# A two-layer convolution kernel on Trainium2: reordering the passage from the last attention region to the last convolution stage

## The chip, the cores and the metric

The kernel runs on one core of one Trainium2 chip. Its metric is the device time of a whole execution, in microseconds; lower is better. The core has TensorE (PE) for matrix products, VectorE (DVE), ScalarE (ACT) and GpSimd (POOL) for the rest, SyncE (SP) that mostly issues transfers, and 16 DMA engines that move data between HBM and the on-chip memory.

## The reference, cut to what matters

The input x is (4, 128, 128, 128): four images, 128 channels, 128 x 128 pixels, float32. Layer 0 is region attention followed by a convolutional MLP:

```python
reg = x[:, :, ih, iw]                       # 9 x 9 overlapping regions of 16 x 16 pixels, step 14
y = _ln(tok, ln1_g, ln1_b); qkv = y @ w_qkv # per region
attn = softmax(q @ k^T * hd ** -0.5)        # 4 heads of 32
tok = attn @ v @ w_out + b_out + tok
merged = out / cnt                          # regions added back, seams divided by their count
xf = merged                                 # (b, h*w, c)
y = _ln(xf, ln2_g, ln2_b) @ w_p0 + b_p0     # 128 -> 256 channels
ym = depthwise 5x5 convolution of y
ym = batchnorm(ym)                          # statistics over all images and pixels
y = gelu(gelu(ym)) @ w_p2 + b_p2 + xf
```

Layer 1 is two 3x3 convolutions of quantised activations and weights, each with a batch norm, and a residual. It is not touched by the change.

## The kernel before, in words

**Tiling.** Each image is nine bands of sixteen rows (two of them shared with the next band), so there are T = 36 bands over four images. One pass of the loop over t works on one band of nine regions: slot j = 0 to 8 runs the scores, exponentials and values of region j, and lists beside them pieces of other work. These are the first norm and projections of a later band (`ln1_chunks`, called a1 and a2), the tail of the band before (`post_chunks`, b1 and b2: output projection `wo`, residual, second norm, the projection `wp0` called p0 in lines L511 and L640, and the stores of its result y), and steps of an earlier image's 5x5 depthwise convolution. `beside(t)` returns the plan: which of these pieces stand in which slot. PE, ACT, DVE and SP run their instructions exactly in the order in which the program lists them; only POOL's order is left to a scheduler.

**A tail.** `post_begin` (L592, L593, L595) adds and halves the seams of the band's attention output `ob`. `project` multiplies by `wo` (L511) and adds the residual into `xf` (L622). The norm squares on ACT (L444), sums over channels on PE (L450), forms the variance (ACT L456, DVE L457, and L460, which clips it at zero), takes Ln and Exp on ACT (L464, L465), spreads the result over all channels and multiplies on DVE into `xn` (L494). In most tails the spreading goes through a DMA; in the last one it is four products with a selector matrix on PE (L477), which `selector` (L429) copies from the identity. Four p0 pieces for each block, one for each half of the channels (h) and of the rows (hh), multiply by `wp0`. ACT evicts each into a y tile with even and odd columns taken apart (L640), of which there are two for each h, used in turn, and SP stores it to `y_d` in HBM (L504). A y tile is free again when its store has landed.

**The last attention band** (t = T-1 = 35). After its nine slots the loop lists the last region's values (L952, L960 on PE, reciprocal L972 and products L974, L976 on DVE, the seam's addition L979 on POOL), then `post_begin` on DVE, then the p0 pieces left over from the previous band's second block, and then the tail of the last band by `beside(T)`.

**The late stage** (`conv_rest`, L773). The rest of the last image's depthwise convolution is 24 tiles. A tile takes input rows u from `y_d` in up to eight row groups: one main transfer on SP and two halo transfers on POOL (`fill`, L692), and its band matrices w by POOL (L667). Input tiles are three from the attention stage (`ut_`), three new ones (`ur`) and one of the `ob` tiles, so seven tiles are loaded ahead. What doesn't depend on the last tail is loaded before `beside(T)`, the remaining row groups after it. Each tile's products (L678) go to two score banks in PSUM, used in turn; ACT copies each half to a `cr` tile (L821), DVE takes its batch-norm statistics from `cr` (L827), and SP and ACT store one half each to `cv_d` (L830). After the fourth tile from the end SP issues `first_loads`: for the first two units of the gelu stage, 1 MB of `cv` (L199) and 0.5 MB of `xfl` (L206) each. When the last tile is copied, DVE aggregates the statistics (L184) and forms the batch norm's scale and shift (L1114 to L1120), and ACT begins with gelu (L1304).

Of the kernel before, what the change touches and what calls it, by code (L numbers as in the profile page):

```python
# [48 lines left out]
def layers(  # L49
# [56 lines left out]
    vectors, used = const.tile([P, 25], F32, name="vectors"), [0]  # L106
# [16 lines left out]
    eps_t, mhalf, qb, quad = vectors[:, 17:18], vectors[:, 18:20], vectors[:, 20:21], vectors[:, 21:25]  # L123
    nc.vector.memset(eps_t, LN_EPS)
# [70 lines left out]
    def load(n):  # L195
        b, k = pixel_units[n]
        cv = ld[0].tile([P, 2, U], F32, name="cv")
        src, px = (cv_d[b][k // 2], pixels(k % 2)) if b < B - 1 else (cv_d[b], pixels(k))
        nc.sync.dma_start(out=cv, in_=src.rearrange("(h p) n -> p h n", p=P)[:, :, px])  # L199
        loaded[n] = [cv]  # L200

    def load_xf(n):
        b, k = pixel_units[n]
        xf = ld[0].tile([P, U], F32, name="xfl")
        if b < B - 1:
            nc.sync.dma_start(out=xf, in_=xf_d[b][:, pixels(k)])  # L206
        else:
            nc.sync.dma_start(
# [5 lines left out]
    def first_loads():  # L214
        for n in range(2):
            load(n)
            load_xf(n)

    with ExitStack() as actx:
# [205 lines left out]
        def selector(room):  # L425
# [3 lines left out]
            nc.vector.tensor_copy(  # L429
# [4 lines left out]
        def normalise(src, n, sel=None):  # L434
# [11 lines left out]
            def variance():  # L446
# [9 lines left out]
                nc.scalar.activation(rstd, ps[:, 0, :w], AF.Square, scale=1.0 / P)  # L456
                nc.vector.scalar_tensor_tensor(  # L457
# [41 lines left out]
        def store(out, in_):  # L499
            stores.append((out, in_))  # L500

        def flush(n, engine=nc.sync):
            for out, in_ in stores[:n]:
                engine.dma_start(out=out, in_=in_)  # L504
# [81 lines left out]
        def post_begin(t, engine=nc.gpsimd):  # L586
            b, i = bands[t]
            rows = RS if i == NR - 1 else STEP

            o = ob[t]  # L590
            if i:
                engine.tensor_tensor(o[:, 0:2, :], o[:, 0:2, :], ob[t - 1][:, RS - 2 :, :], ALU.add)  # L592
                engine.tensor_scalar(o[:, 0:2, :], o[:, 0:2, :], 0.5, 1.0, ALU.mult, ALU.mult)  # L593
            seam = o[:, :rows, STEP : STEP * NR].rearrange("p r (j c) -> p r j c", c=STEP)[:, :, :, 0:2]
            engine.tensor_scalar(seam, seam, 0.5, 1.0, ALU.mult, ALU.mult)  # L595
# [8 lines left out]
        def post_chunks(t, sel=None):  # L604
# [4 lines left out]
            for at, (r, n) in enumerate(finished(t)):  # L609
# [24 lines left out]
                def p0(h, hh, r=r, n=n // 2, held=held):  # L634
# [3 lines left out]
                    y = y2t[h].pop(0)  # L638
                    y2t[h].append(y)
                    nc.scalar.activation(  # L640
                        y[:, :n],
                        pm[:, : n * P].rearrange("p (r c e) -> p r e c", r=n, e=2),
                        AF.Identity, bias=bp0[:, h : h + 1],
                    )
                    cut = min(n, GR - (row + 2) % GR)
                    for a, z in ((0, cut), (cut, n)):
                        if z > a:
# [3 lines left out]
                                y[:, a:z].rearrange("p r e x -> p (r e) x"),  # L651
                            )
# [120 lines left out]
        def conv_rest(n, pool, next_loads):  # L773
# [11 lines left out]
            U, W = {}, {}  # L785
# [13 lines left out]
            us += [pool.tile([P, 32 * CW], F32, name=f"ur{n_}") for n_ in range(3)]  # L799
            us.append(op.tile([P, RS, P], F32, name="ob").rearrange("p r c -> p (r c)"))  # L800
            ws += [pool.tile([P, 3, 8, 32], F32, name=f"wr{n_}") for n_ in range(3)]

            for at in range(ahead):
                if at >= len(ut_):
                    nc.gpsimd.memset(us[0], 0.0)
                if tiles[at][2] == 0 and len(W) >= len(wt_):
                    nc.gpsimd.memset(ws[0], 0.0)
                begin(at)
                load(at, 0, tiles[at][3] - 1, halo=False)
                load(at, 0, tiles[at][3] - 2, main=False)  # L810
            for t in ws[: len(ws) - len(W)]:
                nc.gpsimd.memset(t, 0.0)

            def step(at):
# [3 lines left out]
                depthwise(pc, W[k, jj][:, :, c:], U[at], 4 * nj)  # L818
                for half in range(2):
                    cv = pool.tile([P, nj * ng, CW], F32, name="cr", bufs=7)  # L820
                    nc.scalar.copy(  # L821
                        cv.rearrange("p n x -> p (n x)"), pc[half].rearrange("p j g x -> p (j g x)")
                    )
# [675 lines left out]
```

## Time and profile before

| | us |
|---|---|
| median of 3 runs | 3064.66 (3064.0 to 3068.08) |
| profiled execution | 3063.26 |
| its span, first to last instruction | 3061.5 |
| PE busy | 2951.9 (96%) |
| DVE busy | 2023.4 (66%) |
| ACT busy | 1986.0 (65%) |
| POOL busy | 1025.5 (33%) |

The mean clock granted to PE is 0.988 of full speed. Times inside the kernel are counted from the start of the span. The page cuts the span into 40 slices of 76.5 us and gives a digit for each engine and slice, the busy share in tenths; the passage of which this document speaks lies from about 1984 to 2125 us, most of it in the slices that begin at 1990 and 2066 us. A timeline line gives start and duration of a group of instructions, engine, line of the kernel, operation, tiles, and in brackets how long the engine was idle before it and what ended the wait. A window line gives busy time and instruction count of PE, weight loads, DVE, ACT and POOL, the PE clock, the mean busy share of the DMA engines and GB/s.

### The profile page before, as it was taken

How to read it: one execution, taken by the hardware profiler on the slowest of the kernel's cores; microseconds unless marked ns; L12 is line 12 of the kernel's file. 1: busy time of each engine (PE TensorE's matmuls, PEld its weight loads, DVE VectorE, ACT ScalarE, POOL GpSimd, SP SyncE). 2: the span in 40 equal slices, each digit the busy share in tenths (PEclk: the TensorE clock that was granted, in tenths of full speed). 3: DMA queues.
4: the chain of work that ended last, by engine and by line, in shares of the span. 5: the costliest groups of instructions: out<-in, count | busy, mean ns of one | idle time of the engine just before them, and what ended most of it. 6: DMA issues, size and time to landing. Idle time of an engine off the chain costs nothing.

```text
span 3061.5 us, 87377 instructions
## 1 busy us (share of the span) xinstructions
PE 2951.9 (96%) x36860; PEld 1406.8 (46%) x36860; DVE 2023.4 (66%) x3184; ACT 1986.0 (65%) x2643; POOL 1025.5 (33%) x1370
## 2 busy tenths in 40 slices
PE   7999999999999999999999999977999999999998
PEld 4545554444444444444444444533444444444443
DVE  4877898777777777776676667735555555666543
ACT  5778787777777777777766677634677666333343
POOL 5444445444444444444344444452111111000000
PEclk9999999999999999999999999989999999999999
DMA  7455776777776677777688787789999997551498
GB/s 164 130 154 171 187 186 176 204 220 221 210 215 188 181 213 213 214 220 203 175 237 237 207 229 207 224 269 314 359 359 358 356 340 234 165 158 43 163 360 302
DMA packets 720636, 686.14 MB, mean 224 GB/s; under 512 B 512065, under 2 KB 599434, under 8 KB 712554
## 3 DMA queue, kind: packets, MB, share of 16 engines
q1 hardware_dynamic: 701802, 644.90, 69.8%
q0 software_dynamic: 12832, 28.74, 3.3%
q10 hardware_dynamic: 5600, 6.80, 0.6%
q8 instruction: 293, 4.80, 0.6%
q14 instruction: 109, 0.89, 0.1%
HBM read 408.72 MB, written 275.51 MB: 223 GB/s over the span
## 4 chain that ended last, share of the span: by engine, by line
PE 82%; DMA 5%; DVE 4%; ACT 4%; issue 3%; POOL 1%; SPq 1%; ACTq 0%; DVEq 0%; POOLq 0%
PE pc L1267 22%; PE pm L511 18%; PE sc L889 9%; PE po L952 9%; PE pm L678 9%; PE pb L1316 7%; PE po L960 4%; PE pm L450 3%; DMA y_d<-y 2%; DVE rd L972 2%; ACT pt L897 1%; ACT v L880 1%; DVE xn L494 1%; DVE xf L622 0%; DMA u<-in_L_conv_w_dram 0%
## 5 line engine op out<-in xcount | busy, mean ns | idle before, releaser
L972 DVE RECIPROCAL rd<-po 128x256 f32<-128x256 f32 x324 | 568.8, 1755 | 386.1 <-PE po L960 382.5
L897 ACT ACTIVATE pt<-sc 128x1024 f32<-128x1024 f32 x648 | 628.4, 1025 | 119.1 <-PE sc L889 63.0
L1267 PE MATMUL pc<-q,wq 128*128 128x512 fp8e4 x3168 | 699.2, 380 | 5.1 <-DVE q L1279 5.1
L907 POOL TENSOR_TENSOR sm<-pt 128x512 f32<-128x512 f32 x324 | 414.7, 1280 | 673.4 <-ACT pt L897 451.4
L1267 PEld LDWEIGHTS <-wq 128*128 128x128 fp8e4 x3168 | 309.1, 98 | 405.6 <-issue 42.4
L889 PE MATMUL sc<-q,kr 32*128 32x256 f32 x5184 | 389.6, 402 | 17.7 <-ACT pt L897 17.2
L889 PEld LDWEIGHTS sc<-q,kr 32*128 32x128 f32 x5184 | 241.1, 183 | 271.9 <-issue 181.7
L952 PE MATMUL po<-pt,v 128*32 128x256 f32 x5184 | 350.3, 388 | 9.8 <-DVE part L976 9.0
L678 PE MATMUL pm<-u,w 64*32 64x504 f32 (+3 forms) x5376 | 290.2, 558 | 0.0
L907 DVE TENSOR_TENSOR sm<-pt 128x512 f32<-128x512 f32 x324 | 249.0, 768 | 22.3 <-ACT pt L897 22.3
L511 PE MATMUL pm<-xn,wqkv 128*32 128x512 f32 (+1 forms) x2304 | 247.1, 551 | 1.8
L511 PE MATMUL pm<-xn,wp 128*32 128x512 f32 (+1 forms) x2304 | 241.5, 548 | 7.1 <-ACT y L640 4.4
L640 ACT ACTIVATE y<-pm,vectors 128x512 f32<-128x512 f32 (+1 forms) x288 | 182.8, 641 | 93.9 <-PE pm L511 54.8
L1316 PE MATMUL pb<-cv,wp 128*128 128x512 f32 x512 | 233.6, 599 | 8.4 <-ACT cv L1307 8.4
L1275 DVE BATCH_NORM_STATS2 st<-pc 128x6 f32<-128x512 f32 x256 | 165.8, 690 | 84.2 <-PE pc L1267 84.2
L742 ACT COPY c<-pm 128x512 f32<-128x512 f32 x208 | 111.9, 590 | 164.7 <-PE pm L678 164.5
L952 PEld LDWEIGHTS po<-pt,v 128*32 128x32 f32 x5184 | 138.2, 109 | 174.7 <-issue 81.0
L979 POOL TENSOR_TENSOR ob<-ob,part 128x32 f32<-128x32 f32 x288 | 128.7, 447 | 229.7 <-DVE part L976 216.7
L960 PE MATMUL po<-sm,ones 128*32 128x256 f32 x2592 | 203.6, 382 | 1.9 <-POOL sm L907 1.9
L1329 POOL TENSOR_SCALAR a<-y 128x1024 f32<-128x1024 f32 x64 | 66.5, 1039 | 394.3 <-DVE y L1324 394.3
L1324 DVE SCALAR_TENSOR_TENSOR y<-pb,vectors,xfl 128x512 f32<-128x512 f32 x128 | 90.3, 747 | 140.9 <-PE pb L1316 136.1
L511 PE MATMUL pm<-wqkv,yr 128*32 128x128 f32 x5184 | 176.7, 274 | 0.0
(186 smaller groups left out, 3730.6 us busy)
## 6 DMA issues: line engine op xcount, KB each, us to landing
cv<-cv_d SPq DMA_DIRECT2D x64, 1024.0 KB
u<-y_d SPq DMA_DIRECT2D x96, 560.0 KB
cv_d<-c SPq DMA_DIRECT2D x208, 256.0 KB
xn<-row SPq DMA_DIRECT2D x76, 512.0 KB
y_d<-y SPq DMA_DIRECT2D x136, 256.0 KB
xfl<-xf_d SPq DMA_DIRECT2D x64, 512.0 KB
id_d<-y SPq DMA_DIRECT2D x64, 512.0 KB
idt<-id_d SPq DMA_DIRECT2D x64, 512.0 KB
```

Of the source, the lines that this page charges most:

```text
L511: nc.tensor.matmul(out[m], w[:, m], v, start=True, stop=True)
L640: nc.scalar.activation(y[:, :n], pm[:, : n * P].rearrange("p (r c e) -> p r e c", r=n, e=2), AF.Identity, bias=bp0[:, h : h + 1],)
L678: nc.tensor.matmul(outs[half][32 * q : 32 * q + 32, j, :, a:z], wt[hs, s, c, :], ut[hs, :, c, a + s - 1 : z + s - 1], start=(s == 1), stop ...
L889: nc.tensor.matmul(sc[h // 2][:, h % 2, kc, :].rearrange("p (r c) -> p r c", c=RS), region(kr, j)[hs, kc * P : (kc + 1) * P], queries(j, h ...
L897: nc.scalar.activation(pt, sc[p], AF.Exp)
L907: add(sm, pt[:, :, 0, :], pt[:, :, 1, :], ALU.add)
L952: nc.tensor.matmul(po[hs, 0, :], v[:, kc, hs], pt[h // 2][:, h % 2, kc, :], start=(kc == 0), stop=(kc == 1),)
L960: nc.tensor.matmul(po[hs, 1, :], ones, sm[h // 2][:, h % 2, :], start=True, stop=True)
L972: nc.vector.reciprocal(rd, po[:, 1, :])
L1267: nc.tensor.matmul(pc[:, h], w[:, t, :], q1[b][:, rows, dx : dx + P], start=(t == 0), stop=(t == 8),)
L1275: nc.vector.bn_stats(st[:, 2 * n + h, :], pc[:, h])
L1316: nc.tensor.matmul(pb[:, m], wp2[:, h, :], cv[:, h, px], start=(h == 0), stop=(h == 1))
```

## The change

It has seven parts.

1. In the last region (t = 35, j = 8), the first two p0 pieces of the first block stand ahead of `values(8)`, and `post_begin` follows on DVE; then come the scaling of the second block's xn, the other two p0 pieces, and the second block's. The seam's addition of this region is done by DVE. In this band the convolution step of slot 8 stands in slot 4.
2. `post_begin` on DVE halves by a tensor_tensor with a vector of 0.5. Where the selector is used, variance and square of the mean are put into a maximum in PSUM, and then subtracted, in place of a subtraction and a maximum with zero; the selector is copied by ACT.
3. In the last tail, the p0 pieces with hh = 1 have y tiles of their own (pool `rp`, name `xr`). Those with h = 1 are evicted by DVE and stored through ACT's queue, those with h = 0 as before.
4. The loads of the first three late tiles that don't depend on the last tail are issued in slot 8 (`first`), those of tiles 3 to 6 before the last tail (`more`). Of the first three, two of the row groups remain for afterwards, of the others one.
5. The statistics of the late stage are taken from the score bank in PSUM.
6. The last three late tiles are copied into input tiles that are spent.
7. `first_loads` is issued through ACT's queue ahead of the late stage's products.

```diff
             o = ob[t]
             if i:
...
-                engine.tensor_scalar(o[:, 0:2, :], o[:, 0:2, :], 0.5, 1.0, ALU.mult, ALU.mult)
+                halved(o[:, 0:2, :])
...
+                if sel is not None:
+                    nc.vector.scalar_tensor_tensor(
+                        ps[:, 1, :w], ps[:, 1, :w], 1.0 / P, rstd, ALU.mult, ALU.max
+                    )
+                    nc.vector.tensor_tensor(rstd, ps[:, 1, :w], rstd, ALU.subtract)
+                    return
...
+            def halved(part):
+                if engine is nc.gpsimd:
+                    engine.tensor_scalar(part, part, 0.5, 1.0, ALU.mult, ALU.mult)
+                else:
+                    spread_ = [[0, n] for n in part.shape[1:]]
+                    half = bass.AP(phalf.tensor, phalf.offset, [phalf.ap[0], *spread_])
+                    engine.tensor_tensor(part, part, half, ALU.mult)
...
+                    if t == T - 1 and hh:
+                        if h == 0:
+                            held["y"] = rp.tile([P, LB * P], F32, name="xr")
+                        y = held["y"][:, h * LB * P // 2 : (h + 1) * LB * P // 2].rearrange(
+                            "p (r e x) -> p r e x", r=RB, e=2
+                        )
+                    else:
+                        y = y2t[h].pop(0)
+                        y2t[h].append(y)
...
+                    bias, engine = bp0[:, h : h + 1], nc.sync
+                    if t == T - 1 and h:
+                        engine = nc.scalar
+                        nc.vector.tensor_scalar(y[:, :n], by_column, bias, None, ALU.add)
+                    else:
+                        nc.scalar.activation(y[:, :n], by_column, AF.Identity, bias=bias)
...
+            open_ = lambda at: 2 if at < len(ut_) else 1
+
+            def first(at):
+                begin(at)
+                ng = tiles[at][3] - open_(at)
+                load(at, 0, ng, halo=False)
+                load(at, 0, ng - 1, main=False)
...
+                    if at < len(tiles) - 3:
+                        cv = late["pool"].tile([P, 8 * CW], F32, name="cr", bufs=7)
+                    else:
+                        spent = done[at - 3].rearrange("p g c x -> p (g c x)")
+                        cv = spent[:, half * 8 * CW : (half + 1) * 8 * CW]
+                    pc_ = pc[half].rearrange("p j g x -> p (j g x)")
+                    nc.scalar.copy(cv, pc_)
...
-                            st0[:, k, half, at_, unit, :], cv[:, 4 * j : 4 * j + 4].rearrange("p n x -> p (n x)")
+                            st0[:, k, half, at_, unit, :], pc_[:, 4 * CW * j : 4 * CW * (j + 1)]
...
-                    if at == len(tiles) - 4:
-                        next_loads()
...
             if t == T:
                 return [
                     *b1[:2], *b2[:2], b1[2], b1[3], b2[2], b2[3], b1[4], b2[4],
-                    b1[5], b2[5], b1[6], *b1[7:], b2[6], *b2[7:],
+                    b1[5], b1[6], b2[5], b2[6], *b1[7:], *b2[7:],
                 ]
...
+            if t == T - 1:
+                order = (1, 5, 3, 7, 4, 6, 2, 0)
...
+                    if t == T - 1 and j == NR - 1:
+                        first, more, rest = conv_rest(len(units) - 1)
+                        for at in range(len(ut_)):
+                            first(at)
+                        halves(j)
+                        values_in(j)
+                        run([*side[2][:2], side[1][1]])
+                        values(j)
+                        post_begin(t, nc.vector)
+                        run([side[1][0], *side[2][2:]])
+                        break
...
-            last()
             flush(len(stores))
-            post_begin(T - 1, nc.vector)
...
-            rest = conv_rest(len(units) - 1, late, first_loads)
-            run(beside(T, selector(late.tile([P, 4 * P], F32, name="sel"))))
+            more(late)
+            run(beside(T, selector(late.tile([P, 4 * P], F32, name="sel"), nc.scalar.copy)))
             flush(len(stores))
+            first_loads()
             rest()
```

## The prediction

> **What bounds the kernel now.** I read the page's engine table and slices first, then the chain that ended last around the place of the change, then engine timelines, the table of waits and the windows there. The page says that the span is TensorE's (PE), except near 2000-2030 us:
>
> ```profile
> PE 2951.9 (96%) x36860; PEld 1406.8 (46%) x36860; DVE 2023.4 (66%) x3184; ACT 1986.0 (65%) x2643; POOL 1025.5 (33%) x1370
> PE   7999999999999999999999999977999999999998
> PE 82%; DMA 5%; DVE 4%; ACT 4%; issue 3%; POOL 1%; SPq 1%; ACTq 0%; DVEq 0%; POOLq 0%
> ```
>
> Each slice is 76.5 us; the two 7s (1990-2143 us) are the passage from the last attention region through the last tail to the late stage's convolution. All that the change moves lies there, so I work on that stretch alone. The timelines of DVE, then ACT, then PE (start, duration, idle before and its releaser) show three stalls:
>
> ```profile
> 1995.61 0.30 DVE L595 TENSOR_SCALAR ob<-ob 128x256 f32<-128x256 f32 x1
> 2001.51 3.26 DVE L460 TENSOR_SCALAR rstd<-rstd 128x256 f32<-128x256 f32 x1
> 2005.13 0.50 DVE L460 TENSOR_SCALAR rstd<-rstd 128x256 f32<-128x256 f32 x1
> ...
> 2004.81 0.51 ACT L464 ACTIVATE rstd<-rstd,vectors 128x256 f32<-128x256 f32 x1 [1.70 <-DVE rstd L460]
> 2020.33 0.69 ACT L640 ACTIVATE y<-pm,vectors 128x512 f32<-128x512 f32 x1 [4.05 <-DMA y_d<-y]
> 2115.83 1.07 ACT L821 COPY cr<-sc 128x512 f32<-128x512 f32 x2 [5.62 <-DMA xfl<-xf_d]
> ...
> 1996.05 3.64 PE L511 MATMUL pm<-ob,wo 128*32 128x512 f32 x32 [1.83 <-DVE ob L595]
> 2005.82 6.13 PE L477 MATMUL pm<-rstd,sel 128*128 128x256 f32 x16 [3.16 <-ACT rstd L465]
> 2011.88 6.22 PE L511 MATMUL pm<-xn,wp 128*32 128x512 f32 x56
> 2029.45 10.79 PE L678 MATMUL sc<-u,w 64*32 64x512 f32 x138 [6.45 <-DMA u<-y_d]
> ```
>
> One L460 takes 3.26 us where its twin takes 0.50. A y eviction waits 4.05 us for a store to free its tile. The last two copies of the convolution wait 5.62 us behind the first loads of the gelu stage. The convolution starts at 2029.45, when the last y store has landed (2026.97 on the chain) and a halo load, 2.0-2.1 us to landing, has followed it. Then the windows, whose last columns are clock, DMA share and GB/s:
>
> ```profile
> 2016.00:2020.00 4.00, 2.10 (x20) 0.39 (x12) 0.00 (x0) 0.28 (x1) 0.00 (x0) 1.00 1.05 318
> 2020.00:2024.00 4.00, 1.94 (x8) 0.20 (x8) 0.00 (x0) 2.75 (x4) 0.00 (x0) 0.62 0.93 226
> 2024.00:2028.00 4.00, 0.00 (x0) 0.00 (x0) 0.00 (x0) 0.00 (x0) 0.73 (x2) 0.50 0.66 166
> 2028.00:2032.00 4.00, 2.55 (x21) 0.58 (x29) 0.00 (x0) 0.00 (x0) 4.00 (x8) 0.50 0.50 141
> 2032.00:2036.00 4.00, 4.00 (x64) 1.40 (x56) 0.00 (x0) 0.36 (x1) 3.51 (x8) 0.67 0.22 60
> 2036.00:2040.00 4.00, 4.00 (x85) 1.50 (x72) 2.61 (x8) 1.78 (x4) 1.57 (x3) 1.00 0.73 228
> 2044.00:2048.00 4.00, 4.00 (x112) 2.12 (x103) 3.87 (x16) 1.43 (x3) 2.09 (x5) 1.00 1.05 360
> ```
>
> The DMA engines are full up to 2024, have a hole of about 7.6 us (4 x (0.34 + 0.50 + 0.78 + 0.27)) from 2024 to 2040, and are full again up to 2104, where tiles come every 3.6 us against 2.55-2.8 us of PE work. So the stage is bound by transfers on both sides of the hole.
>
> **What the Trainium skill says.** "SBUF — State Buffer", Who interferes with whom: a tensor_scalar on DVE can take a port pair that it shares with GpSimd, and whoever comes second waits for the other's whole instruction; an operation with at most one SBUF input outside these modes doesn't. The trace agrees: POOL (GpSimd) is busy 4.00 of 4.00 us in 2000-2004, with memsets and descriptors, and L460 takes 3.26. "DMA: Bandwidth & Descriptors", Issuing engines are not separate DMA queues: SP and ACT feed the same 16 engines; and Queues, rings and completion order there: each engine goes round-robin between its queues by packets. No stretch of this trace shows two large queues side by side. Its Specifications put line rate at 512 bytes or more: the y stores, rows of 256 bytes, run at 226 GB/s with DMA 0.93 busy, the convolution's loads at 360. "TensorE: Matmul & The Clock Gate", What's actually happening: after some idle windows the clock halves; here it is 0.50 in 2024-2032.
>
> **The change part by part**, against the profiled execution (3063.26 us, 3061.5 of span and 1.76 around it; the runs have a median of 3064.66, 1.4 above it).
>
> *Listing of the last region.* values(8) goes ahead of two of b1's p0 (16 matmuls at 6.22/56 = 0.111 us, 1.8), so it ends near 1989.7 instead of 1991.46, where the other block's p0 begin. DVE follows with rows of before: reciprocal 1.74, products 0.39 and 0.18, seam 0.3 (now DVE), post_begin 0.43 + 0.29 + 0.30, then xn 0.69: 4.3 us, and 0.4 of handovers, to 1994.4. PE has the two p0 until 1991.5, waits 2.9, then does the other block's four p0 (2.7, as at 1991.46-1994.2 before) and comes to wo at 1997.1 instead of 1996.05: **+1.1**, bounds -1.8 (the wait for L595 gone, nothing in its place) and +2. The convolution step that moves from slot 8 to 4 is 2.7-2.8 us of PE in a stretch where PE has no idle, here as there: 0, bounds -1 and +1.
>
> *rstd.* Max and subtract now read PSUM, so one SBUF input each; 0.42 as L457. ACT, in order, has its second L456 until 2003.10, so L464 starts there instead of 2004.81: **-1.7**. If the shorter idle keeps the clock from falling at 2003.9, L477 (6.13 us at half speed) takes about 3: bound -4.7. The selector's copy on ACT (0.42 on DVE) falls in ACT's idle of 3.49 us before L444: 0; without that cover, 0.4.
>
> *y in own tiles, two engines, two queues.* Removes the 4.05 us. p0 starts at 2011.88 + 1.1 - 1.7 = 2011.3; 64 matmuls at 0.111 are 7.1 us, the last eviction (0.69) ends near 2019.2 instead of 2023.81: -4.6. What is late next is the store's landing. The stores are 2 MB, at 226 GB/s 9.2 us of full DMA; from the first issue (2013.7) with some 2 us to land that is 2025 at the earliest, while prefetches still share the engines. So at most 2 of the 4.6 us arrive.
>
> *First loads.* cv and xfl for two units (3 MB) are issued by ACT right behind its y stores, and the built program puts the third unit's cv (1 MB) on SP ahead of the remaining main rows of the first convolution tiles, its xfl behind them: 4.5 MB in all, at 360 GB/s 12.5 us of DMA. Before they ran at 2105-2124, beside the convolution's end. The hole holds 7.6 us. ACT's loads take packets from the last y stores: landing moves from a possible 2025 to 2025-2030, I take 2027.5, which is +0.5 on 2026.97. Then tile 0's remaining rows queue on SP behind 1 MB that shares with ACT: 5.5 us at half of 360 GB/s, of which 2-3 are over before the y landing. The first convolution matmul comes near 2031.8: **+2.3** on 2029.45 (this holds the three parts above). Behind it on SP: the third xfl waits for ACT's second, and the first result's store and tile 7's load come after it. The load of 4.5 MB is through by about 2038, so the full DMA period starts later by these 2.3 us and isn't longer. Bounds: 2025 for the stores with the loads covered, -4.6; uncovered, 12.5 - 7.6 + 2.3 = +7.
>
> *The in-chain issue* of the first three tiles' loads: before they were issued at 1989-2005, and DMA was 0.88-1.04 busy there apart from 2000-2004 (0.53). 0; bounds -1.9 (that gap filled) and +0.5.
>
> *Statistics from PSUM.* Copy and bn_stats now read one bank and alternate by program order: 0.58 + 0.75 + 0.58 + 0.75 and handovers, about 2.9 us from a tile's last matmul until its bank is free, where the copies alone took 1.07. Under tiles 3.6 us apart that is hidden; the last four at 2.55-2.6 lose 0.3 each: **+1.2**, bounds 0 and 24 x 0.35 = 8.4 if no tile were bound by DMA.
>
> *End of the convolution.* The last tiles go to spent buffers and no load stands before their stores. Before: last matmul 2111.64, last bn_aggr 2119.1, 7.5 us. After: 2.9 + 1.32 (L184) = 4.2: **-3.3**, bounds -4.5 and -2. The chain from there to gelu (BN affine, 5.5 us from L184 to L1304) is unchanged, and its ACT table load (1.28) lies beside DVE's work.
>
> Sum: 2.3 + 1.2 - 3.3 = **+0.2**, 3063.5 on the profile; on the median of the runs about 3064.9; I say 3065.
>
> **The rivals.** *Loads hidden, landing early:* the hole takes all, the stores land at 2025 and the SP load is over by then, first matmul 2027 (-2.4), or 2025 with the clock kept (-4.6); with -3.3 and no loss in the banks, -5.7 to -7.9: about 3058. For it: 7.6 us of hole, 18 us between 2020 and 2038. Against: stores at 226 GB/s. *Slower:* the 4 MB ahead on two queues starve the 256-byte stores and the first tiles' rows, which PE waits for; at 1 packet of 4 KB to one of 256 bytes the stores land only when ACT's loads (8.3 us) are through, 2030-2032, and the SP load follows: first matmul 2036-2039, +7 to +10, sum +5 to +8, 3070-3073. It decides from a first matmul later than 2037.7, where the sum passes +6.1. For it: each of the stores' packets is small, and several SP issues also wait for ACT's transfers. Against: half of the stores are issued before the loads. *Moved wait only:* the rows of the stall vanish and the store wait reappears before the convolution, its start within 1 us of before; then -2 from the last copies, 3062.7. This counts as no change.
>
> **How the numbers follow.** The measurement can tell about 0.2% (6.1 us). My forecast has 0.42 and the moved wait 0.13. Loads hidden has 0.22, of which 0.16 passes -6.1. Starved stores have 0.23, of which 0.22 passes +6.1 (the bound of the banks, 8.4, counted there). What doesn't pass joins the middle: 0.16 / 0.62 / 0.22. The range leaves out about 0.1 at either end: 3057.5, nearly the hidden case, to 3074, starved stores and banks together.
>
> **What would show it.** L460 gone and the new pair at 0.3-0.6 us; no y eviction waiting on a store; wo's wait at 2.5-3 us behind xn; first convolution matmul near 2031.8 waiting for a load behind cv; DMA share 0.9 and more over 2024-2036; ACT copies alternating with bn_stats; the last bn_aggr about 4.2 us after the last matmul. The forecast is wrong if the first matmul stands before 2027 or after 2037, or if the convolution's tiles are further apart than 3.6 us.

## The result and the profile after

The changed kernel takes 3079.97 us (median of 6 runs, 3074.51 to 3081.03) against 3066.04 us for the kernel before, measured beside it (6 runs, 3062.22 to 3068.4): a ratio of 1.0044, 95% interval 1.0031 to 1.0057. It is about 14 us slower. Its profiled execution took 3080.01 us with a span of 3078.1.

The page of the changed kernel, the lines that answer to those shown of before (busy time and share of each engine; PE's busy tenths in 40 slices; shares of the chain that ended last):

```profile
PE 2954.3 (96%) x36860; PEld 1408.6 (46%) x36860; DVE 2025.9 (66%) x3189; ACT 1984.9 (64%) x2640; POOL 1025.1 (33%) x1369
PE   7999999999999999999999999967999999999998
PE 82%; DVE 5%; DMA 5%; ACT 4%; issue 3%; SPq 0%; POOL 0%; ACTq 0%; DVEq 0%; POOLq 0%
```

PE has the same work; a 7 became a 6. The timeline of PE in the changed kernel (start, duration, in brackets the idle time before and its releaser; L519 was L511, L485 was L477, L704 was L678):

```profile
1997.98 4.48 PE L519 MATMUL pm<-xn,wp 128*32 128x384 f32 x32 [2.87 <-issue]
2003.74 2.78 PE L519 MATMUL pm<-ob,wo 128*32 128x512 f32 x24 [0.42 <-ACT y L669]
2010.84 3.72 PE L485 MATMUL pm<-rstd,sel 128*128 128x256 f32 x16 [1.35 <-ACT rstd L473]
2014.49 7.07 PE L519 MATMUL pm<-xn,wp 128*32 128x512 f32 x64
2045.49 4.93 PE L704 MATMUL sc<-u,w 64*32 64x512 f32 x48 [23.93 <-DMA u<-y_d]
```

The last p0 ran without a stop (7.07 us for 64 matmuls), and ended at 2021.57 against 2023.00 before. Then PE stood still for 23.93 us: the late convolution began at 2045.49, not 2029.45. To compare executions without what differs earlier (2.5 us here), I count from the first exponential of the last band (1939.06 us before, 1941.57 after):

| us from the first exponential of the last band | before | after | difference |
|---|---|---|---|
| last wo begins | 57.00 | 60.68 | +3.7 |
| last p0 ends | 83.95 | 80.00 | -4.0 |
| first late convolution matmul | 90.39 | 103.92 | +13.5 |
| last late convolution matmul | 172.58 | 187.26 | +14.7 |
| last bn_aggr ends | 180.03 | 191.42 | +11.4 |
| first gelu | 185.56 | 197.19 | +11.6 |
| end of the span | 1122.40 | 1136.55 | +14.2 |

So the loss lies between the last p0 and the first late matmul: 6.45 us before, 23.93 after. The end of the convolution gave 3.3 us back. The 2.5 us between gelu and the end are not in all executions of kernels with the same gelu stage (from 936.3 to 940.6 us in those below), and I read nothing from them.

What PE waited for shows in the queues of the changed kernel: the timeline of ACT, SP and POOL (queue entries are DMA issues; most of them take 0.3 to 0.6 us here, and a longer one holds a wait):

```profile
2015.63 0.69 ACT L669 ACTIVATE y<-pm,vectors 128x512 f32<-128x512 f32 x1 [3.77 <-PE pm L519]
2022.42 1.61 ACTq L512 DMA_DIRECT2D y_d<-xr  x2
2024.07 1.50 ACTq L201 DMA_DIRECT2D cv<-cv_d  x1
2025.60 1.44 ACTq L208 DMA_DIRECT2D xfl<-xf_d  x1
...
2020.93 0.37 SPq L512 DMA_DIRECT2D y_d<-y  x1
2023.99 5.09 SPq L512 DMA_DIRECT2D y_d<-xr  x2
2029.17 0.53 SPq L201 DMA_DIRECT2D cv<-cv_d  x1
2031.79 4.63 SPq L718 DMA_DIRECT2D u<-y_d  x3
...
2029.32 0.58 POOL L718 DMA_DIRECT2D u<-y_d  x1 [21.24 <-DMA y_d<-xr]
2041.15 1.68 POOL L718 DMA_DIRECT2D u<-y_d  x3 [8.86 <-issue]
```

Two things are late. The first is the issue of SP's stores. ACT's first y was evicted by 2016.32, but SP issued its store at 2020.93. In the trace that store has the same semaphore as ACT's first store (issued at 2017.40), and it waited until that one had landed, at 2020.87. SP's last store waited in the same way for ACT's last, which landed at 2028.70; this wait is most of the 5.09 us. The second is the landing of this last store. ACT's loads, issued from 2024.07, are then in flight, and the store landed only at 2040.64. POOL could issue the second halo of the first late tile, which needs it, at 2041.15.

### The profile page after: what moved, and what is told of

Same layout as the page of the kernel before. It is cut to its first block, busy times and chain, and to the rows that moved or that the text cites. A ratio compares the mean times of both kernels' runs of the same rounds, so it can differ in the third digit from the quotient of the medians.

```text
span 3078.1 us, 87373 instructions
## 1 busy us (share of the span) xinstructions
PE 2954.3 (96%) x36860; PEld 1408.6 (46%) x36860; DVE 2025.9 (66%) x3189; ACT 1984.9 (64%) x2640; POOL 1025.1 (33%) x1369
## 4 chain that ended last, share of the span: by engine, by line
PE 82%; DVE 5%; DMA 5%; ACT 4%; issue 3%; SPq 0%; POOL 0%; ACTq 0%; DVEq 0%; POOLq 0%
PE pc L1315 22%; PE pm L519 18%; PE sc L924 9%; PE po L987 9%; PE pm L704 9%; PE pb L1364 7%; PE po L995 4%; PE pm L452 3%; DMA y_d<-y 2%; DVE rd L1007 2%; ACT pt L932 1%; ACT v L915 1%; PE sc L704 1%; DVE xn L502 1%; DVE xf L638 1%
## 5 line engine op out<-in xcount | busy, mean ns | idle before, releaser
L987 PE MATMUL po<-pt,v 128*32 128x256 f32 x5184 | 350.2, 388 | 10.7 <-DVE part L1011 10.1
L704 PE MATMUL pm<-u,w 64*32 64x504 f32 (+3 forms) x5376 | 290.8, 558 | 0.4 <-DVE xf L638 0.4
L519 PE MATMUL pm<-xn,wqkv 128*32 128x512 f32 (+1 forms) x2304 | 247.7, 551 | 2.2 <-issue 0.4
L519 PE MATMUL pm<-xn,wp 128*32 128x512 f32 (+1 forms) x2304 | 242.1, 550 | 6.2 <-issue 2.9
L519 PE MATMUL pm<-wqkv,yr 128*32 128x128 f32 x5184 | 176.5, 274 | 0.0
```

Source lines behind the costliest of these rows:

```text
L519: nc.tensor.matmul(out[m], w[:, m], v, start=True, stop=True)
L704: nc.tensor.matmul(outs[half][32 * q : 32 * q + 32, j, :, a:z], wt[hs, s, c, :], ut[hs, :, c, a + s - 1 : z + s - 1], start=(s == 1), stop ...
L987: nc.tensor.matmul(po[hs, 0, :], v[:, kc, hs], pt[h // 2][:, h % 2, kc, :], start=(kc == 0), stop=(kc == 1),)
```

## The experiments

All times below are medians with the ratio to the kernel before. The runs of before that the first four were sent with, and those of the later ones, spread widely (3058.16 to 3076.53 us, medians 3065.9 to 3066.9), so a difference below some 3 us is read from the traces, in the same frame as above.

A trace is one execution, and not always one near the median: that of the run with the first tile's halos through ACT is the slowest of its 20. Executions also differ ahead of the edits. In the changed kernel and the four runs that differ from it only behind the last tail, the last p0 ended between 78.78 and 83.07. In the latest of them, the first run below, the clock granted to PE was 0.58 in 2012-2016, where the changed kernel had 1.00. So the distance from the last p0 to the first late matmul (6.45 us before, 23.93 after) is a steadier measure of what the loads and stores cost.

### The loads at their old place

```diff
-            load(n, nc.scalar)
-            load_xf(n, nc.scalar)
+            load(n)
+            load_xf(n)
...
+                    if at == len(tiles) - 4:
+                        next_loads()
...
-            first_loads()
-            rest()
+            rest(first_loads)
```

> The changed kernel, with the first loads put back behind the fourth tile from the end of the late convolution, on SP's queue (part 7 undone, all else kept). Theory A (the loads hold back the last y stores, which the first convolution tile needs): the last store lands near 2027-2030 instead of 2041, the first late matmul stands at 2028-2032 instead of 2045.5, and the time is 3060-3067, that is -13 to -18 on the changed kernel and within 3 us of the kernel before. Theory B (the other parts cost it: wo comes 6.2 us later, and the y stores on two queues wait for each other): the first matmul stays later than 2038 and the time above 3071.

Measured: 3075.69 us, ratio 1.0032 (1.002 to 1.0045); 4.3 us less than the changed kernel. The first late matmul moved from 103.92 to 96.11, which is somewhat over half of the way in theory A, and 5.7 us short of before. But 3 us of what is missing stand ahead of the end of the last p0, where nothing was edited: the distance from there fell from 23.93 to 13.04, so that the loads cost 10.9 of the 17.5 us by which the change had lengthened it. At the other end 3.5 us were given back: the last aggregation came 7.69 us after the last late matmul, as in the kernel before, and not 4.16. So both theories hold in part: the loads are the larger part of the standstill, but in the time, after what they give back, they are the smaller part. The view of the DMA engines for 2020 to 2024 us of this run (busy share in slices, GB/s, packets, queues; q10 is ACT's, q1 SP's) shows what else is wrong:

```profile
DMA  0000029877877777860300798899989999888888
GB/s 0 0 0 0 0 72 230 223 218 218 220 215 218 218 218 215 218 133 8 82 0 18 177 223 200 205 223 223 215 192 192 195 256 256 215 220 220 220 202 192
q10 hardware_dynamic: 2080, 0.52, 53.5%
q1 hardware_dynamic: 477, 0.12, 12.1%
```

With two queues and no loads the engines are idle until 2020.5, then mostly 0.7 to 0.8 busy with ACT's stores, and nearly idle again just before 2022.2, while evicted tiles wait: SP's first store was issued at 2022.26, 3.7 us after its eviction. From then on they are mostly 0.8 to 0.9 busy.

### The loads early in the kernel before

```diff
-                    if at == len(tiles) - 4:
-                        next_loads()
...
+            first_loads()
             rest()
```

`first_loads` issues through ACT's queue here, as in the change.

> The kernel before, with the first loads alone moved: issued through ACT's queue ahead of the late stage's products. Theory A: the loads alone do it; first late matmul at 2036-2043 instead of 2029.5, time +8 to +14 on the kernel before. Theory B: all y stores are on SP here and are issued before the loads or next to them, so that nothing is held back by more than the shared bandwidth; first matmul by 2033, time 0 to +3.

Measured: 3070.9 us (20 runs), ratio 1.0017 (1.001 to 1.0024). The first late matmul stood at 100.49, 10.1 us later than before, and the distance from the last p0 was 17.09 us, 10.6 more; theory A said so. But 4.1 us came back at the end (bn_aggr 3.31 us after the last matmul), so that the time is +4 and not the +8 to +14 of theory A. The timeline of PE:

```profile
2046.01 4.41 PE L678 MATMUL sc<-u,w 64*32 64x512 f32 x44 [17.09 <-DMA u<-y_d]
```

The DMA view of this run, first 2026 to 2030 us, with the y stores alone, then 2032 to 2036, with ACT's loads beside them:

```profile
DMA packets 3470, 0.88 MB, mean 219 GB/s; under 512 B 3470, under 2 KB 3470, under 8 KB 3470
q1 hardware_dynamic: 3470, 0.88, 90.2%
...
q10 hardware_dynamic: 293, 1.13, 89.0%
q1 hardware_dynamic: 288, 0.07, 7.9%
```

This is the starving, counted: 288 packets of SP's queue against 293 of ACT's in the same 4 us. The Trainium skill says in "DMA: Bandwidth & Descriptors", Queues, rings and completion order, that each engine goes round-robin between its queues and moves a whole packet, typically of several descriptors, before it switches. The equal counts agree with taking turns; how many rows make a turn, they can't tell. A packet of ACT's, as the profile counts them, is 4 KB and one of SP's 256 bytes, so SP's share of the bytes is a sixteenth, and its rate falls from 3470 packets to 288. In the changed kernel, 2030 to 2034 us, SP's queue gets still less:

```profile
q10 hardware_dynamic: 331, 1.26, 93.3%
q1 hardware_dynamic: 123, 0.03, 3.2%
```

Here SP had no row of a store under way for about one of the four us (2031 to 2032). The 512 packets of its last store began at 2032.3 and ended at 2040.0, and in that time 470 of ACT's 4 KB packets went beside them: again about one to one, until nearly all of ACT's loads were through.

### The loads early on SP's queue, and behind the first tile

The first is the changed kernel without the engine argument in `first_loads`; the second keeps ACT's queue, but calls `next_loads` behind the tile `at == 0`.

> The changed kernel, with the first loads at the changed place but on SP's queue, behind the y stores and ahead of the first tiles' remaining rows. If the stores are held back by the other queue's large packets taking turns with theirs (theory A1), they now land by 2030 and not at 2041; the rows stand behind 4 MB in one queue (11 us), and the first late matmul comes at 2038-2043; time 3072-3078. If it is only the amount of data that is moved ahead, whatever the queue (A2), the last store lands near 2038-2041 again, and the time is 3078-3082.

Measured: 3078.42 us, ratio 1.0048 (1.0031 to 1.0065). The y stores were through when POOL issued its second halos, at 2031.42, where the changed kernel had 2041.15:

```profile
2031.42 1.68 POOL L718 DMA_DIRECT2D u<-y_d  x3
```

So A1 holds for the stores. The tiles' rows were behind the loads instead, and the first late matmul came at 102.02, 1.9 earlier than as changed. In either queue 4 MB ahead of rows that PE waits for cost about the same.

> The changed kernel, with the first loads on ACT's queue as changed, but issued behind the first tile of the late convolution. Theory A: stores and first tiles are free, first late matmul at 2028-2032; the 4.5 MB then fall partly into the DMA's hole and partly into its full period, so that the convolution ends 3-8 us later than with the loads at its end; time 3064-3071. Theory B: first matmul later than 2038, time above 3071.

Measured: 3084.96 us, ratio 1.0071 (1.0054 to 1.0088), the slowest of all. The first late matmul stood at 92.01 (2033.46 us in this trace, somewhat later than theory A's 2028 to 2032), and the distance from the last p0 was 13.23 us, as with the loads at their old place. But the convolution took 97.13 us from there, against 83.34 as changed: 13.8 us for the loads in a stretch with full DMA, more than I gave it.

### The stores of the last tail on one queue

On top of the loads at their old place:

```diff
                     if t == T - 1 and h:
-                        engine = nc.scalar
                         nc.vector.tensor_scalar(y[:, :n], by_column, bias, None, ALU.add)
```

> The changed kernel with the first loads back at their old place on SP (as in the run before of that name) and, added to it, all y stores of the last tail on SP's queue; own y tiles and DVE's evictions are kept. Theory C (with the loads gone, it is the two queues that cost: a store on one queue is issued only when an earlier one on the other has landed, because they share a semaphore): the last store lands 4-5 us after the last eviction instead of 7.5, the first late matmul 3-5 us earlier than with two queues (13 us after the last p0 there, 8-10 here), time 3071-3073. Rival D (it is the lack of DMA rate for rows of 256 bytes, whichever queue): the distance from the last p0 to the first late matmul stays within 1 us of 13, time 3075-3077.

Measured: 3067.62 us (12 runs), ratio 1.0003 (0.9993 to 1.0012): 8 us less than with two queues, more than theory C had. From the last p0 to the first late matmul it is 8.85 us (13.04 with two queues), which theory C foretold, and the first late matmul stands at 88.01. But the last store landed 6.39 us after the last p0, against 7.45 with two queues, a smaller gain than theory C had, and POOL's first halo, which waits for stores, came at 5.75 us, against 7.54. So the stores account for 1.1 to 1.8 us of the 4.2. The DMA view for 2020 to 2024 us of this run, nearly full from end to end:

```profile
DMA  9896548998999999999898888999888887888999
q1 hardware_dynamic: 3400, 0.86, 90.4%
```

The rest stands in POOL's order, which a scheduler makes. The timelines of POOL, first with two queues (loads at their old place), then with one:

```profile
2031.31 0.58 POOL L718 DMA_DIRECT2D u<-y_d  x1 [24.56 <-DMA y_d<-xr]
2032.04 1.14 POOL L718 DMA_DIRECT2D u<-y_d  x2 [0.15 <-issue]
2033.18 1.11 POOL L718 DMA_DIRECT2D ur<-y_d  x2
2034.29 1.68 POOL L718 DMA_DIRECT2D u<-y_d  x3
...
2027.76 3.43 POOL L717 DMA_DIRECT2D u<-y_d  x6 [19.05 <-DMA y_d<-xr]
```

With one queue the two remaining halos of the first late tile are POOL's first and third of these transfers, and by the semaphores the first matmul waits only for the first. With two queues they are the first and the sixth, with halos of four other tiles between them, and the first matmul waits for both. The sixth landed at 2036.56, where POOL's first had landed at 2034.37 and the main rows at 2032.75. That is 2.2 us. To test it I took POOL's order out: on top of the loads at their old place, with two queues, the first tile's halos go through ACT's queue.

```diff
-                    load(at, tiles[at][3] - m - 1, m + 1, main=False)
+                    load(at, tiles[at][3] - m - 1, m + 1, main=False, by=nc.gpsimd if at else nc.scalar)
```

> The changed kernel with the loads at their old place (as in the first experiment, y stores on two queues), and the two remaining halos of the first late tile issued through ACT's queue, not in POOL's order. Theory I (with two queues POOL's scheduler puts this tile's second halo behind five others, and that is 2-3 us of the 4.2 that two queues cost between the last p0 and the first late matmul): the distance, 13.0 us there, falls to 10-11, as with one queue plus the later landing of the stores. Theory C (the stores wait for each other, and that is all): it stays at 12-13. The time by theory I 3071-3074, by theory C 3074-3077.

Measured: 3072.59 us (20 runs), ratio 1.0018 (1.0011 to 1.0026). The distance from the last p0 to the first late matmul is 10.91 us, 2.1 less, as theory I has it. The intervals of the two ratios touch, so the time alone doesn't show it. The timeline of PE in this run:

```profile
2024.71 7.07 PE L519 MATMUL pm<-xn,wp 128*32 128x512 f32 x64
2042.69 7.80 PE L704 MATMUL sc<-u,w 64*32 64x512 f32 x88 [10.91 <-DMA u<-y_d]
```

The same part alone on the kernel before (own y tiles, DVE's evictions, ACT's queue for h = 1; the diff is that of the change for `p0`, `store` and `flush`):

> The kernel before, with part 3 alone: own y tiles, evictions by DVE for h = 1, and these stored through ACT's queue. Theory C: the 4 us of waiting for a y tile go, but the stores on one queue wait for landings on the other; first late matmul 3-6 us later than before (in the frame of the passage), time +2 to +6. If instead the two queues only cost in company with the new listing or the early loads, the first late matmul is at the place of before or up to 2 us earlier, and the time 0 to -2.

Measured: 3074.73 us (20 runs), ratio 1.0026 (1.0017 to 1.0034): +8, above the forecast. The first late matmul is at 94.70, 4.3 later than before, and comes 9.74 us after the last p0 (6.45 before). The place is in theory C's range, but not for its reason alone: the last store landed only 0.9 us later than before (89.30 against 88.45). POOL's order has changed here too. Its timelines, first before, then in this run:

```profile
2027.27 3.27 POOL L692 DMA_DIRECT2D u<-y_d  x6 [18.71 <-DMA y_d<-y]
...
2033.70 0.57 POOL L702 DMA_DIRECT2D u<-y_d  x1 [20.54 <-issue]
2034.43 1.10 POOL L702 DMA_DIRECT2D u<-y_d  x2 [0.16 <-issue]
2035.53 1.63 POOL L702 DMA_DIRECT2D ur<-y_d  x3
2037.14 1.63 POOL L702 DMA_DIRECT2D u<-y_d  x3
```

The first matmul waits here for POOL's seventh transfer, which landed at 2039.09, 2.8 us after its first (2036.26); before it waited only for the first. So about two thirds of the 4.3 us are POOL's order, and most of the rest is the later first halo. In all traces with the stores on two queues and these halos on POOL, the tile's second one stands sixth or seventh, in all with one queue third or fourth. Why the scheduler does so stays open.

The traces of both pairs show 4 to 5 us at the first gelu, the medians 8; what the other 3 are is open.

### The old listing

Besides the last edit (stores on SP, loads at their old place), the last slot, its convolution step and the place of the first three tiles' loads are those of before:

```diff
-            if t == T - 1:
-                order = (1, 5, 3, 7, 4, 6, 2, 0)
...
-                    if t == T - 1 and j == NR - 1:
...
+            last()
             flush(len(stores))
+            post_begin(T - 1, nc.vector)
```

> As the run with the stores on SP, and the listing of the last region, its convolution slots and the place of the first tiles' loads are those of before as well (parts 1 and 4 undone); kept are the tensor_tensor forms, own y tiles with DVE's evictions, statistics from PSUM and spent tiles. Theory E (the listing delays the output projection by some 4 us and the DMA work of that stretch starts later): wo at 1996-1998 instead of 2001.8, first late matmul 3-4 us earlier than with the new listing, time 3066-3070. Rival F (the tail has slack, since the stores wait for the DMA anyway): wo earlier, but the first late matmul within 1.5 us, time 3071-3073.

Measured: 3066.82 us (20 runs), ratio 1.0003 (0.9995 to 1.0011), the same as without the edit. In the trace wo came 3.9 us earlier (56.45 against 60.31) and the last p0 4.0, but the first late matmul only 1.3 (86.74): the stores absorbed it, rival F. The convolution ended 4 us earlier all the same, since it took 86.07 us in the trace without this edit and 83.34 here. The medians do not confirm that, so I compared the two listings once more, on the best of the versions below:

> As the run with statistics from SBUF and the loads last, with the listing of the last region, its slots and the early issue of the first three tiles' loads as changed (parts 1 and 4 back in). Theory E: the output projection comes 4 us later, and the late convolution with it, +3 to +5 on that run (3060-3062). Rival F: the y stores are bound by the DMA and absorb it, first late matmul within 1.5 us, time within 1.5 us (3056-3059).

Measured: 3062.43 us (12 runs), ratio 0.9985 (0.9973 to 0.9998), against 3057.43 with the old listing. In the trace wo came 4.8 us later, the first late matmul 2.0 and the first gelu 2.3. So a third to under half of the later wo reached the late stage. In the medians the new listing costs 0.8 us in one pair and 5.0 in the other; the traces show 1.3 and 2.0 at the first late matmul, and its size stays open.

### The loads behind the last tile

```diff
-                    if at == len(tiles) - 4:
+                    if at == len(tiles) - 1:
                         next_loads()
```

> As the run with the old listing, and the first loads are issued on SP behind the last tile of the late convolution instead of the fourth from the end. If the stores of the last tiles wait behind these loads (the 5.6 us before the last copy in the kernel before, 4.1 in the run with the loads back in place), the last aggregation comes 4.2-4.5 us after the last late matmul instead of 7.5, and the time falls by 3 to 4 us, to 3063-3066; the loads end about 12 us after their issue, and the first gelu needs only the first 1 MB of them. If the gelu stage waits for them instead, the gain is given back and the time is the same as with the old listing.

Measured: 3063.49 us (12 runs), ratio 0.9989 (0.9981 to 0.9998), 3.3 us less than without it, as forecast. The last aggregation comes 4.17 us after the last matmul (7.20 without).

> The kernel before with one edit: the first loads behind the last tile of the late convolution instead of the fourth from the end. If the wait of 5.6 us before the last copies belongs to them, the last aggregation comes 3.4-4.2 us after the last matmul instead of 7.5, and the time is 3-4 us lower than before. If the gelu stage then waits for its loads, the first gelu stands where it was, and the time too.

Measured, this one edit on the kernel before: 3061.46 us (20 runs), ratio 0.9986 (0.9978 to 0.9994). The aggregation comes 3.32 us after the last matmul instead of 7.45; the first gelu, 185.56 before, is at 179.51, so the gelu stage does not wait for its loads. The timeline of ACT in this run, with the last copies 1.49 us after the one before, where they had waited 5.62:

```profile
2110.87 1.07 ACT L821 COPY cr<-sc 128x512 f32<-128x512 f32 x2 [1.49 <-PE sc L678]
2113.43 1.07 ACT L821 COPY cr<-sc 128x512 f32<-128x512 f32 x2 [1.49 <-PE sc L678]
```

The copies still go to `cr` tiles here, so the spent tiles (part 6) weren't needed for it.

### Statistics from SBUF

On top of the old listing and the loads last:

```diff
-                            st0[:, k, half, at_, unit, :], pc_[:, 4 * CW * j : 4 * CW * (j + 1)]
+                            st0[:, k, half, at_, unit, :], cv[:, 4 * CW * j : 4 * CW * (j + 1)]
```

> As the run with the loads last, and the late statistics are taken from the copies in SBUF as before (part 5 undone). Statistics from PSUM alternate with the copies and hold a score bank 2.9 us instead of 1.1. If that costs (my estimate was 1.2 us), the late convolution from first to last matmul is 1-2 us shorter here and the time 1 us lower; the end from the last matmul to the last aggregation is about the same. If the full DMA hides all of it, both are the same within 0.5 us.

Measured: 3057.43 us (11 runs), ratio 0.9972 (0.9962 to 0.9981), the fastest of all, 6 us less than with the statistics from PSUM, where the forecast had 1. In the trace the convolution from first to last matmul is 81.83 us (84.65), and the aggregation 3.36 us after it (4.17): 3.6 us in all. The timelines of ACT at the end, first with the statistics from PSUM, then in this run:

```profile
2118.86 0.59 ACT L859 COPY ob<-sc 128x512 f32<-128x512 f32 x1 [0.72 <-PE sc L703]
2120.28 0.59 ACT L859 COPY ob<-sc 128x512 f32<-128x512 f32 x1 [0.83 <-DVE st L863]
```

```profile
2113.16 1.07 ACT L859 COPY ob<-sc 128x512 f32<-128x512 f32 x2 [1.49 <-PE sc L703]
```

The control for POOL's order, on this version, where it is the good one already:

> The fastest version (old listing, stores on SP, loads last, statistics from SBUF) with the same edit for the first tile's halos. There POOL has this tile's second halo third. Theory I: at most 0.5-1 us earlier at the first late matmul, time 3056-3058, the same. If ACT's queue by itself is quicker than POOL's issue, 1-2 us earlier, 3055-3056.

Measured: 3060.67 us (14 runs), ratio 0.9981 (0.9972 to 0.999), not told from the version without the edit; its first late matmul is 1.3 us earlier (86.80). That is more than theory I allowed, but the last y store had already landed 1.2 us earlier (84.40 against 85.64), ahead of the edited transfers. In both traces the first matmul waited for the main rows and not for a halo, so the control shows no gain of ACT's queue by itself.

Last, the statistics from PSUM on the kernel before:

> The kernel before, with the late stage's statistics read from the score bank in PSUM (part 5 alone). Theory G (copies and statistics alternate on one bank, 2.9 us for a tile against 1.1, and the convolution has too little slack): the late convolution takes 2.5-4 us longer from first to last matmul, time +3 to +6 on before. Rival H (the full DMA hides it, and the 6 us between the two last runs are drift): within 1 us of before in both.

Measured, part 5 alone on the kernel before: 3068.04 us (12 runs), ratio 1.0004 (0.9992 to 1.0016), which tells nothing. Its trace has the convolution 1.9 us longer, below theory G's range, and the first gelu 3.5 us later, of which 1.2 stand ahead of the convolution. All traces together say more than the pairs. In the eight with statistics from PSUM (the one with loads inside the convolution left out) it took 83.15 to 86.07 us, in the seven with statistics from SBUF 80.12 to 82.19. The means are 2.6 us apart. With the 0.8 us at the last aggregation (4.17 against 3.36) that is about 3.4 us; the medians of the two pairs say 6 and 1.

## Why the prediction was wrong

It said 3065.0 (3057.5 to 3074), and the time is 3080. The step that failed is the place of the first late matmul: +2.3 us forecast, +13.5 measured. The end of the last p0 gave 4.0 us, and the distance from there grew by 17.5. By the runs above, 10.9 of these are the early loads and 4.2 the two store queues with the order of POOL's halos; for the remaining 2.4 no run takes out a cause. Along its own steps:

- **Listing of the last region.** The wait for xn was forecast as 2.9 us and was 2.87. But wo came 3.7 us later, not 1.1: two y evictions ahead of it waited 1.50 and 1.39 us for their tiles, and the p0 after the wait ran at a lower clock (PE clock 0.82 in 1996-2000, 4.48 us for 32 matmuls against 2.76). That step failed too; the late stage got half of it or less.
- **rstd.** Right: L460 and its successor take 0.43 and 0.42 us, and Ln follows its engine's own Square at once. L477's successor ran at full clock, 3.72 us for 6.13, which is towards the bound that I gave; in two of the later runs with the same tail it took 5.3 to 5.4.
- **y in own tiles.** The evictions gained 4.0 of the forecast 4.6 us. "At most 2 of the 4.6 us arrive" failed too: none did at the first late matmul with two queues. I took the stores as bound by 226 GB/s in whichever queue, and named the waits of one queue for the other only in a rival, without a price: 1.1 to 1.8 us. That POOL's order of halos could change with the queues I did not consider: 2.1 us by the run that takes the order out, 2.2 and 2.8 by the landings. Alone this part costs 8 us in the medians (4.3 at the first late matmul).
- **First loads.** +2.3 forecast for the first late matmul, +13.5 measured; the loads' share is 10.9 in the distance from the last p0 by putting them back, 10.6 alone on the kernel before. What failed inside it is the landing of the y stores, taken as 2027.5 with a bound of 2030; the last landed at 2040.64. For this number I had worked out no way in which the two queues share the engines, and they share turns. The rival "slower" had this mechanism, and its 2030 to 2032 came from 8.3 us of loads. But their packets moved only from 2028.7, behind ACT's own stores, to 2040.6, and the last of SP's stores, issued at 2028.71, went beside them all the way. The rival had 0.23, and even its first matmul (+7 to +10) was too early.
- **Statistics from PSUM.** +1.2 forecast within 0 and 8.4; the traces say 2.6 between first and last matmul. The alternation came as forecast, and its price was too low.
- **End of the convolution.** -3.3 forecast, 7.45 to 4.16 measured, -3.3. So the number is right, and the reason half: the loads' new place alone does it, without the spent tiles, and statistics from SBUF bring the distance to 3.3 or 3.4 us.

Undone one after another, the losses in the medians are 4.3 us for the loads (after what they give back at the end), 8.1 for two queues, 0.8 for the listing (5.0 in the other pair) and 6.1 for the statistics beside 3.3 gained by the loads at the end; the remainder (norm, own y tiles, evictions by DVE) is left in the fastest version. What it is worth isn't told: the intervals of that version and of the single edit with the loads last on the kernel before (0.9962 to 0.9981 and 0.9978 to 0.9994) overlap.

## What to carry to other kernels

Price a moved load in packets and not in bytes: beside a queue of 4 KB packets, the queue of 256-byte packets got as many packets and a sixteenth of the bytes here, and what waited for its last packet waited for nearly all of the other queue. Ask what a second queue brings where the DMA engines are near full, and what it takes: here its transfers shared semaphores with the first queue's, and an issue then waited for the other queue's landing. Where a scheduler orders one engine's issues, see in the trace what a change elsewhere does to that order; here that cost more than the waits. One line, the first loads behind the last tile and not behind the fourth from the end, gave some 4 us (ratio 0.9986), while the whole reordering lost 14.

## What the runs showed of the hardware that I had not expected

Two queues took turns one to one, 288 packets to 293 in 4 us, and the smaller one's rate fell from 0.88 MB to 0.07 MB in that time. A convolution whose tiles come about every 3.4 us, with PE at work for 2.8 of them, still felt about 2.8 us of alternating copies and statistics on each tile's banks: 2.6 us over its 24 tiles, in the mean of eight traces against seven.
